# Q, K and V as 49 products of 128 x 128 x 128, and layer norms normalised on ScalarE

## The chip, the cores and the metric

The kernel runs on one core of a Trainium2 chip. A core has a matrix engine (PE in the profile, with the loads of its stationary operand shown apart as PEld), VectorE (DVE), ScalarE (ACT), GpSimd (POOL) and SyncE (SP), which here only starts transfers between HBM and the on-chip SBUF. Matrix products land in PSUM banks of 128 x 512 fp32 and are read from there by DVE or ACT. The metric is the device time of one execution in microseconds.

## The reference

128 graphs of 64 nodes with 512 features pass through four layers, each of the form `x = layernorm(x + layer(x, adj))`, all in fp32: a hypergraph convolution (512 to 1024 to 512), an attention-like layer with one 512 x 512 weight, three graph convolutions of 512 x 512, and graph attention with 8 heads of 64. The change lies in the last one, and in the layer norms of all four:

```python
qkv = (x @ W_qkv).reshape(B, N, HEADS, 3, DIM_HEAD)
q, k, v = (jnp.transpose(qkv[..., i, :], (0, 2, 1, 3)) for i in range(3))
dots = jnp.einsum('bhid,bhjd->bhij', q, k) * scale
...
out = jnp.einsum('bhij,bhjd->bhid', attn, v)
return out @ W_out + b_out
```

## The kernel before

Sixteen groups of 8 graphs (512 rows of `x`, held as four pairs of 128 x 512) go through all layers. In the steady state three groups are in the kernel at once, each in another part of it: `first_half` of group q+1 ("a" in the order lists), the layers of `second_half` of group q ("b"), and the attention's tail of group q-1 ("t", the later part of the same generator). The list `order` at the end of the kernel says in which sequence the pieces are written down for each step. That sequence is the priority: a planner then lays out each engine's queue, and takes for an engine the piece of work that is first in it among those whose operands are ready. `behind(key)` forbids that a piece comes before a named instruction of its engine; `strict` holds for the start and the end only.

Every 512 x 512 x 512 product of a group is written as seven products of 256 x 256 x 256 (`multiply`, `product`, line 539) on four quadrants of either operand: B11, B21 and B22 are quadrants or a sum, T1 to T4 sums. `Left.sums` makes the four sums of the activations (lines 518 to 521, DVE). The sums of the weights are made once, in the first group (`Weight.making`, lines 263 to 268), and kept in DRAM by POOL's transfers (line 280). Products accumulate in three PSUM banks out of a pool of four (`ps_acc`); between two accumulations ACT copies a bank away (`snap`, line 555), DVE adds the copies to later products (lines 568, 589, 598) and ACT copies the last quadrant (line 608). For Q, K and V that is three DVE adds and four ACT copies a product. The stationary operand is always 128 x 128 and the moving one has 256 columns.

`Stream` loads the weights on SP's queue in the order of use (`pump`, lines 236 and 238), into a ring of `RING` = 20 slots of 256 KB; a product of a group beyond the first takes seven slots, one after the other. Activations live in the pool `big` (8 slots), the copies of banks and the softmax tiles in `work` (7).

`layer_norm` takes means and variances on DVE (lines 457 and 458), the root on ACT (line 447), the reciprocal on DVE (line 448) and normalises each pair on DVE (line 463). It is used for the four outer layer norms of every group, except l0 and l1 of the first; `late` pairs are normalised in a second call. The hidden layer norm (line 797) has code of its own.

In `second_half`, after the third graph convolution: `agg` adds into `x`, the layer norm `l2`, transposes (line 1186), ACT copies (line 1194), `left.sums()`, the product q with a stop after five of seven, the addition of the output bias to `x` (line 1201), k, the 64 x 64 `scores` (lines 1356 and 1367), then v, the softmax, and so on. The residual and the layer norm `l1` of the group ahead (`a.p2`, `a.ln1`), and the last layer norm of the group behind (`t.ln3`), lie among them in the order list.

## Time and profile before

| | |
|---|---|
| three executions, us | 2732.28, 2733.82 (median), 2734.45 |
| profiled execution: its span, us | 2732.1 |
| instructions | 67,726 |
| PE busy | 2714.7 us, 28,770 matmuls |
| PEld busy | 2347.7 us, 28,770 loads |
| DVE busy | 2077.8 us, 4,111 |
| ACT busy | 803.9 us, 1,440 |
| POOL busy | 38.0 us, 71 |
| DMA | 405.14 MB, mean 148 GB/s |
| granted PE clock | 1.000 |

The span is the profiled execution from its first to its last instruction; it lies 0.2 us under the fastest of the three times and 1.7 us under their median. Busy time is the union of an engine's instructions. Since instructions of one engine overlap in their pipeline, the distance between two starts says more of what one costs than its duration does. One matmul of the program is two instructions on PE, each with its own load of the stationary operand.

### The profile page before, as it was taken

How to read it: one execution, taken by the hardware profiler on the slowest of the kernel's cores; microseconds unless marked ns; L12 is line 12 of the kernel's file. 1: busy time of each engine (PE TensorE's matmuls, PEld its weight loads, DVE VectorE, ACT ScalarE, POOL GpSimd, SP SyncE). 2: the span in 40 equal slices, each digit the busy share in tenths (PEclk: the TensorE clock that was granted, in tenths of full speed). 3: DMA queues.
4: the chain of work that ended last, by engine and by line, in shares of the span. 5: the costliest groups of instructions: out<-in, count | busy, mean ns of one | idle time of the engine just before them, and what ended most of it. 6: DMA issues, size and time to landing. Idle time of an engine off the chain costs nothing.

```text
span 2732.1 us, 67726 instructions
## 1 busy us (share of the span) xinstructions
PE 2714.7 (99%) x28770; PEld 2347.7 (86%) x28770; DVE 2077.8 (76%) x4111; ACT 803.9 (29%) x1440; POOL 38.0 (1%) x71
## 2 busy tenths in 40 slices
PE   9999999999999999999999999999999999999998
PEld 7888888888888888888888888888888888888887
DVE  6878687876877778777786877778677687776766
ACT  3323223232232332323223233232322323233232
POOL 2000000000000000000000000000000000000000
PEclk9999999999999999999999999999999999999999
DMA  7545454454544545455454554545545455454541
GB/s 257 179 129 154 123 175 140 142 162 131 173 131 139 168 129 170 130 145 168 134 165 129 146 165 133 164 129 151 163 130 167 130 154 157 128 166 129 158 125 63
DMA packets 309532, 405.14 MB, mean 148 GB/s; under 512 B 57424, under 2 KB 185456, under 8 KB 309232
## 3 DMA queue, kind: packets, MB, share of 16 engines
q1 hardware_dynamic: 304256, 385.45, 48.2%
q0 software_dynamic: 4832, 15.24, 1.5%
q8 instruction: 228, 3.74, 0.6%
q14 instruction: 72, 0.59, 0.1%
q10 hardware_dynamic: 144, 0.13, 0.0%
HBM read 369.78 MB, written 30.93 MB: 147 GB/s over the span
## 4 chain that ended last, share of the span: by engine, by line
PE 96%; DVE 3%; ACT 1%; issue 0%; DMA 0%; DVEq 0%
PE a_l0w L539 15%; PE b_l0w L539 7%; PE a_l2b L539 4%; PE a_q L539 4%; PE a_k L539 4%; PE a_l2a L539 4%; PE a_v L539 4%; PE c_l0w L539 4%; PE a_l1w L539 4%; PE a_wo L539 4%; PE a_l2c L539 4%; PE gt_l L481 3%; PE gt_l0h L481 2%; PE b_l2a L539 2%; PE b_l1w L539 2%; PE b_l2b L539 2%
## 5 line engine op out<-in xcount | busy, mean ns | idle before, releaser
L539 PE MATMUL a_l0w<-w2w,aT_l0h 128*128 128x256 f32 x720 | 164.3, 381 | 0.0
L457 DVE BATCH_NORM_STATS2 st_l<-x 128x6 f32<-128x512 f32 x244 | 157.9, 676 | 0.6
L539 PEld LDWEIGHTS a_l0w<-w2w,aT_l0h 128*128 128x128 f32 x720 | 135.6, 190 | 18.8
L463 DVE TENSOR_SCALAR x<-x,mv_l,rs_l 128x512 f32<-128x512 f32 x244 | 119.3, 543 | 2.2
L539 PE MATMUL b_l0w<-w2w,s_l0h 128*128 128x256 f32 x480 | 108.5, 379 | 0.0
L783 ACT ACTIVATE h<-h 128x1024 f32<-128x1024 f32 (+1 forms) x58 | 55.0, 948 | 178.5 <-DVE h L598 157.4
L539 PEld LDWEIGHTS b_l0w<-w2w,s_l0h 128*128 128x128 f32 x480 | 91.1, 190 | 12.5
L1140 ACT ACTIVATE aT_h<-gth,gb_col 128x256 f32<-128x256 f32 x124 | 47.2, 491 | 159.0 <-PE gth L1128 159.0
L447 ACT ACTIVATE rs_l<-mv_l,eps_t 128x4 f32<-128x4 f32 (+1 forms) x63 | 18.8, 298 | 252.3 <-DVE mv_l L458 245.0
L492 ACT COPY aT_l<-gt_l 128x512 f32<-128x512 f32 x148 | 78.1, 597 | 46.4 <-PE gt_l L481 46.4
L555 DVE TENSOR_TENSOR u_l0w<-a_l0w,b_bc 128x512 f32<-128x512 f32 x56 | 38.6, 689 | 69.2 <-PE a_l0w L539 69.2
L539 PE MATMUL a_l2b<-gwbw,aT_h 128*128 128x256 f32 x360 | 86.6, 383 | 0.0
L539 PE MATMUL a_l2c<-gwcw,aT_h 128*128 128x256 f32 x360 | 86.3, 382 | 0.0
L539 PE MATMUL a_q<-aT_xT,wqw 128*128 128x256 f32 x360 | 85.1, 379 | 0.5 <-ACT aT_xT L1194 0.5
L539 PE MATMUL a_l1w<-ww,aT_l 128*128 128x256 f32 x360 | 85.1, 379 | 0.2 <-ACT aT_l L492 0.2
L539 PE MATMUL a_l2a<-aT_l,gwaw 128*128 128x256 f32 x360 | 85.0, 379 | 0.0
L539 PE MATMUL a_k<-aT_xT,wkw 128*128 128x256 f32 x360 | 85.0, 379 | 0.0
L539 PE MATMUL a_v<-wvw,aT_xT 128*128 128x256 f32 x336 | 81.1, 384 | 0.5 <-issue 0.5
L539 PE MATMUL a_l0w<-w1aw,aT_l 128*128 128x256 f32 x336 | 80.8, 383 | 0.0
L539 PE MATMUL a_wo<-wow,aT_oT 128*128 128x256 f32 x336 | 79.5, 379 | 0.0
L539 PE MATMUL a_l0w<-w1bw,aT_l 128*128 128x256 f32 x336 | 79.4, 379 | 0.0
L539 PEld LDWEIGHTS a_l2c<-gwcw,aT_h 128*128 128x128 f32 x360 | 67.2, 190 | 11.6 <-ACT u_l2c L555 3.0
(532 smaller groups left out, 6489.0 us busy)
## 6 DMA issues: line engine op xcount, KB each, us to landing
w2w<-w2k SPq DMA_DIRECT2D x210, 256.0 KB, 2.7
x<-in_x_dram SPq DMA_DIRECT2D x15, 1024.0 KB, 5.8
w1aw<-w1ak SPq DMA_DIRECT2D x60, 256.0 KB, 2.7
w1bw<-w1bk SPq DMA_DIRECT2D x60, 256.0 KB, 2.8
ww<-wk SPq DMA_DIRECT2D x60, 256.0 KB, 2.7
gwaw<-gwak SPq DMA_DIRECT2D x60, 256.0 KB, 3.4
gwbw<-gwbk SPq DMA_DIRECT2D x60, 256.0 KB, 2.7
gwcw<-gwck SPq DMA_DIRECT2D x60, 256.0 KB, 2.7
```

The source lines that it names most:

```text
L447: act.activation(rs[:, at], mv[:, at, 1], AF.Sqrt, bias=eps_t)
L457: vec.bn_stats(st, xg[:, p, :])
L463: vec.tensor_scalar(xg[:, p, :], xg[:, p, :], mv[:, p, 0:1], rs[:, p : p + 1], ALU.subtract, ALU.mult)
L481: ten.matmul(ps[g][f * C : (f + 1) * C, c, p, :], src(2 * duo + p)[rows, c0 : c0 + C], mat[rows, 2 * duo + p, :], start=True, stop=True,)
L492: act.copy(o[:, :, :, g, :], ps[g])
L539: ten.matmul(acc[:, blk, :], lhsT, rhs, start=(first and blk == 0 and i == 0), stop=(last and i == n_k - 1), skip_group_check=True,)
L555: last_add[f"{key}.{what}"] = (act.copy(t, ps) if res is None else vec.tensor_add(t, ps, res(m, n))).ins
L783: act.activation(hn, hn, AF.Relu)
L1140: act.activation(o[:, :, h, :], cols, AF.Relu, bias=gb2_col[:, k : k + 1])
```

## The change

Three things change. First, q, k and v of all groups but the first: each of the seven 256-cubed products is itself written as seven products of 128 x 128 x 128, so 49 for a 512-cubed product. They run in two halves (`DEEP`: four of the outer products, then three); a stage is one inner product for all outer products of a half, four or three matmuls side by side in one bank. `deep_stages` interleaves the halves of q, k and v in one sequence of 42 stages. The inner sums of the activations are made on DVE (`more_sums`), those of the weights on POOL in the first group (`make_deep`), which also writes all seven inner operands to DRAM, so that a stage loads one piece of 256 or 192 KB. Each half ends in quadrants of the outer products, in `temps`, and from these DVE makes q, k or v. Second, `layer_norm` normalises with ACT (`Identity` with a scale and a bias for each row) and DVE computes that bias, `shift`. Third, the pools and the order: `RING` 16, `big` 9, `work` 8, scores after the stage (5, T1), and v in three pieces.

```diff
-RING = 20
+RING = 16
+
+DEEP = ((B11, B21, T1, T2), (T3, T4, B22))
+STAGES = (B11, B21, B22, T1, T2, T3, T4)
+
+
+def deep_stages(n):
+
+    order = [(0, s) for s in (B11, B21, T1, T2, B22)]
+    for i in range(n):
+        if i + 1 < n:
+            order += [(i + 1, B11), (i, T3), (i + 1, T1), (i + 1, B21), (i, T4), (i + 1, T2), (i + 1, B22)]
+        else:
+            order += [(i, T3), (i, T4)]
+    return order
...
-    big = ctx.enter_context(tc.tile_pool(name="big", bufs=8))
+    big = ctx.enter_context(tc.tile_pool(name="big", bufs=9))
-    work = ctx.enter_context(tc.tile_pool(name="work", bufs=7))
+    work = ctx.enter_context(tc.tile_pool(name="work", bufs=8))
...
+        def load_deep(self, q, h, s):
+            n = len(DEEP[h])
+            t = wring.tile([P, 2 * Q], FP, name=f"{self.name}d{h}{s}_{q}", tag="wq")[:, : n * P]
+            nc.sync.dma_start(out=t, in_=self.deep_kept[h][:, STAGES.index(s)].rearrange("p r n -> p (r n)"))
+            return t.rearrange("p (r n) -> p r n", r=n)
...
+        def make_deep(self, got):
+
+            self.deep_kept = []
+            for h, rs in enumerate(DEEP):
+                n = len(rs)
+                k = dram.tile([P, 7, n, P], FP, name=f"{self.name}deep{h}", tag=f"{self.name}deep{h}")
+                d = big.tile([P, 4, n, P], FP, name=f"{self.name}deep_{h}", tag="big")
+                for i, r in enumerate(rs):
+                    b = got[r][0].rearrange("p k (n c) -> p k n c", n=2)
+                    nc.gpsimd.tensor_sub(d[:, 0, i], b[:, 0, 1], b[:, 0, 0])
+                    nc.gpsimd.tensor_sub(d[:, 1, i], b[:, 1, 1], d[:, 0, i])
+                    nc.gpsimd.tensor_sub(d[:, 2, i], b[:, 1, 1], b[:, 0, 1])
+                    nc.gpsimd.tensor_sub(d[:, 3, i], b[:, 1, 0], d[:, 1, i])
+                    nc.gpsimd.dma_start(out=k[:, 0:2, i], in_=b[:, :, 0])
+                    nc.gpsimd.dma_start(out=k[:, 2, i], in_=b[:, 1, 1])
+                nc.gpsimd.dma_start(out=k[:, 3:7], in_=d)
+                self.deep_kept.append(k)
...
-                for what, t in (whole | made if self.scaled else made).items():
+                for what, t in (whole | made if self.scaled else {} if self.deep else made).items():
...
+                if self.deep:
+                    self.make_deep(got)
...
-    w_q, w_k, w_v = (Weight(Wqkv, n * D, f"w{'qkv'[n]}") for n in range(3))
+    w_q, w_k, w_v = (Weight(Wqkv, n * D, f"w{'qkv'[n]}", deep=True) for n in range(3))
...
+                if wt.deep and q > 0:
+                    if wt is w_q:
+                        trio = (w_q, w_k, w_v)
+                        self.todo += [(trio[i // 2], q, (i % 2, s), 1) for i, s in deep_stages(6)]
...
+                if wt.deep and q > 0:
+                    self.here[wt, q, what] = wt.load_deep(q, *what)
...
-        rs = rstd(mv, G, key, slice(pairs[0], pairs[-1] + 1))
+        at = slice(pairs[0], pairs[-1] + 1)
+        rs = rstd(mv, G, key, at)
+        shift = small.tile([P, G], FP, name=f"shift_{key}", tag="shift")
+        vec.scalar_tensor_tensor(shift[:, at], mv[:, at, 0], -1.0, rs[:, at], ALU.mult, ALU.mult)
...
-                vec.tensor_scalar(
-                    xg[:, p, :], xg[:, p, :], mv[:, p, 0:1], rs[:, p : p + 1], ALU.subtract, ALU.mult
+                act.activation(
+                    xg[:, p, :], xg[:, p, :], AF.Identity, bias=shift[:, p : p + 1], scale=rs[:, p : p + 1]
                 )
...
+    class Deep:
+        def __init__(self, key):
+            self.key = key
+            self.xs = [big.tile([P, 8, Q], FP, name=f"d{n}_{key}", tag="big") for n in range(2)]
...
+        def sums(self):
+            self.left = {what: self.slot(what) for what in range(7)}
+            a = self.left
+            s3 = a[T3]
+            vec.tensor_add(a[T1], s3, a[T4])
+            vec.tensor_sub(a[T2], a[T1], a[B11])
+            vec.tensor_sub(s3, a[B11], s3)
+            vec.tensor_sub(a[B22], a[B21], a[T2])
+        def more_sums(self):
...
+            for h, rs in enumerate(DEEP):
+                n = len(rs)
+                o = self.xs[h][:, : 2 * n].rearrange("p (r k) (m c) -> p r k m c", k=2, m=2)
+                s1, s2, s4 = ((x3, st)[h][:, i] for i in range(3))
...
+                vec.tensor_add(s1, o[:, :, 0, 1], o[:, :, 1, 1])
+                vec.tensor_sub(s2, s1, o[:, :, 0, 0])
+                vec.tensor_sub(s4, o[:, :, 1, 0], s2)
+                vec.tensor_sub(s3, o[:, :, 0, 0], o[:, :, 0, 1])
+                self.deep.append({
+                    B11: o[:, :, 0, 0], B21: o[:, :, 1, 0], B22: s4, T4: o[:, :, 1, 1], T1: s1, T2: s2, T3: s3,
+                })
+    def deep_multiply(left, jobs, q):
...
+        banks, snaps, temps = {}, {}, {}
+        for at, s in deep_stages(2 * len(jobs)):
+            j, h = divmod(at, 2)
...
+            bank = "a" if s in (B11, T2, T3, T4) else "b" if s == B21 else "c"
+            fresh, last = s in (B11, B21, T1), s in (B21, B22, T4)
+            if fresh:
+                banks[at, bank] = ps_acc.tile([P, 4, P], FP, name=f"{bank}{h}_{key}", tag="acc")
+            ps = banks[at, bank][:, :n]
+            ws = stream.take_deep(wt, q, h, s)
+            for i in range(n):
+                lhsT, rhs = left.deep[h][s][:, i], ws[:, i]
+                if flipped:
+                    lhsT, rhs = rhs, lhsT
+                ten.matmul(ps[:, i], lhsT, rhs, start=fresh and i == 0, stop=last, skip_group_check=True)
+            stream.done(wt, q, (h, s))
+            if (j, h) not in temps:
...
+            def snap(what):
+                t = work.tile([P, 4, P], FP, name=f"{what}{h}_{key}", tag="w")[:, :n]
+                act.copy(t, ps)
+                snaps[at, what] = t
+
+            if s == B11:
+                snap("u1")
+            elif s == T1:
+                snap("u5")
+            elif s == T2:
+                snap("u2")
+            elif s == B21:
+                vec.tensor_add(sub(0, 0), ps, snaps.pop((at, "u1")))
+            elif s == B22:
+                vec.tensor_add(sub(0, 1), ps, snaps.pop((at, "u2")))
+            elif s == T3:
+                snap("u3")
+                vec.tensor_add(sub(1, 1), snaps.pop((at, "u3")), snaps.pop((at, "u5")))
+            else:
+                act.copy(sub(1, 0), ps)
+                r = {what: temps[j, h][:, i] for i, what in enumerate(rs)}
+                if h == 0:
+                    vec.tensor_add(dst(0, 0), r[B11], r[B21])
+                    vec.tensor_add(dst(1, 0), r[B11], r[T2])
+                    last_add[f"{key}.h"] = vec.tensor_add(dst(0, 1), dst(1, 0), r[T1]).ins
+                else:
+                    last_add[f"{key}.d"] = vec.tensor_add(dst(1, 1), dst(0, 1), r[T3]).ins
+                    vec.tensor_add(dst(0, 1), dst(0, 1), r[B22])
+                    vec.tensor_add(r[T4], r[T4], r[T3])
+                    last_add[key] = vec.tensor_add(dst(1, 0), dst(1, 0), r[T4]).ins
+            yield at, s
...
-        left = Left(f"xT_{q}")
+        left = Deep(f"xT_{q}")
...
+        if q > 0:
+            left.more_sums()
...
+        else:
+            gen = deep_multiply(
+                left, ((w_q, turned(qT), f"q_{q}", True), (w_k, turned(kT), f"k_{q}", True), (w_v, nat(v), f"v_{q}", False)), q
+            )
+            until(gen, 0, B22)
             yield "q1"
+            until(gen, 1, T4)
         with behind(f"q_{q}"):
             vec.tensor_add(xg, xg, bo_bc.unsqueeze(1).to_broadcast([P, G, D]))
         yield "q"
...
+        else:
+            until(gen, 2, T4)
             yield "k1"
+            until(gen, 3, T4)
         yield "k"
+        if q > 0:
+            until(gen, 5, T1)
         probs = [scores(g, duo, qT, kT) for duo in range(2)]
         yield "dots"
...
+        else:
+            until(gen, 5, B22)
             yield "v1"
+            until(gen, 5, T3)
+            yield "v2"
+            whole(gen)
         yield "v"
...
-        gen = multiply([left], (w_v, q), nat(v), f"v_{q}", stops=(3, 6))
-        next(gen)
+        until(gen, 5, B22)
...
-        next(gen)
+        until(gen, 5, T3)
...
-        t.v1 a.c1 t.v b.gt t.soft a.w1a1 a.w1a t.soft2 a.resid b.l2a1 b.l2a a.w1b1 t.ptp a.w1b t.pv a.lnh b.l2b1
+        t.v1 a.c1 t.v2 b.gt t.v t.soft a.w1a1 a.w1a t.soft2 a.resid b.l2a1 b.l2a a.w1b1 t.ptp a.w1b t.pv a.lnh b.l2b1
...
-        t.v1 b.gt t.v t.soft t.soft2 b.l2a1 t.ptp b.l2a t.pv t.osum b.l2b1 b.l2b b.gb3 b.gh b.l2c1 b.l2c2 t.o1 b.l2c t.o2 b.agg
+        t.v1 b.gt t.v2 t.v t.soft t.soft2 b.l2a1 t.ptp b.l2a t.pv t.osum b.l2b1 b.l2b b.gb3 b.gh b.l2c1 b.l2c2 t.o1 b.l2c t.o2 b.agg
```

More of the change, by code (lines that the diff above doesn't have):

```diff
@@ L398, in take, with take_deep @@
             return self.here[wt, q][what]
+        def take_deep(self, wt, q, h, s):
+            self.pump()
+            return self.here.pop((wt, q, (h, s)))
         def done(self, wt, q, what):
-            if q > 0:
+            if wt.deep and q > 0:
+                self.held -= 1
+            elif q > 0:
                 self.held -= wt.halves
@@ L526, in sums, with half, slot @@
             return self
+    class Deep:
+        def __init__(self, key):
+            self.key = key
+            self.xs = [big.tile([P, 8, Q], FP, name=f"d{n}_{key}", tag="big") for n in range(2)]
+        def half(self, m):
+            return self.xs[m][:, 0:4, :]
+        def slot(self, what):
+            m, i = next((m, rs.index(what)) for m, rs in enumerate(DEEP) if what in rs)
+            return self.xs[m][:, 2 * i : 2 * i + 2, :]
+        def sums(self):
[7 more added lines that the diff above has]
+        def more_sums(self):
+            x3 = big.tile([P, 4, 4, P], FP, name=f"d2_{self.key}", tag="big")
+            st = sp.tile([P, 3, 3, P], FP, name=f"ds_{self.key}", tag="s")
+            tail = self.xs[1][:, 6:8, :].rearrange("p k m -> p (k m)")[:, : 3 * P].rearrange("p (r m) -> p r m", r=3)
+            self.deep = []
+            for h, rs in enumerate(DEEP):
+                n = len(rs)
+                o = self.xs[h][:, : 2 * n].rearrange("p (r k) (m c) -> p r k m c", k=2, m=2)
+                s1, s2, s4 = ((x3, st)[h][:, i] for i in range(3))
+                s3 = (x3[:, 3], tail)[h]
+                vec.tensor_add(s1, o[:, :, 0, 1], o[:, :, 1, 1])
[5 more added lines that the diff above has]
+                })
@@ L528, in product, with until @@
+    def until(gen, at, s):
+        while next(gen) != (at, s):
+            pass
     def product(acc, lefts, wt_q, what, first, last, flipped):
@@ L1188, in second_half @@
                             )
[L1189 removed]
+            o = left.half(duo).rearrange("p c (a g i) -> p c a g i", a=2, g=2)
             for h in range(2):
```

36 lines of the change are left out of this document (24 added, 12 removed).

## The prediction

> **What bounds the kernel now.** I read the page first, for busy time and for the chain of work that ended last.
>
> ```profile
> span 2732.1 us, 67726 instructions
> PE 2714.7 (99%) x28770; PEld 2347.7 (86%) x28770; DVE 2077.8 (76%) x4111; ACT 803.9 (29%) x1440; POOL 38.0 (1%) x71
> ...
> PE 96%; DVE 3%; ACT 1%; issue 0%; DMA 0%; DVEq 0%
> ```
>
> PE is the path: 96% of the chain, hardly ever idle, at a granted clock of 1.000. So a change is worth what it takes off PE's stream, less the new places where PE has to wait. Second, the timeline of PE and PEld, for what a matmul costs in the stream (start, length, engine, line, count).
>
> ```profile
> 1402.07 1.70 PEld L539 LDWEIGHTS a_q<-aT_xT,wqw 128*128 128x128 f32 x8
> 1403.80 1.70 PEld L539 LDWEIGHTS a_k<-aT_xT,wkw 128*128 128x128 f32 x8
> ...
> 1418.67 0.30 PEld L539 LDWEIGHTS a_v<-wvw,aT_xT 128*128 128x128 f32 x2
> ...
> 14.64 0.54 PEld L127 LDWEIGHTS dps<-atc,ht 64*64 64x64 f32 x16 [0.33 <-issue]
> ...
> 1416.19 0.49 PEld L696 LDWEIGHTS sps<-hb,ht 64*64 64x64 f32 x14 [0.33 <-issue]
> ```
>
> Eight instructions of 256 columns take 1.73 us from start to start, 216 ns each, although a load lasts 190 and a matmul some 380: both overlap their neighbours. The third line is the first pair after a stall: two loads of 190 ns within 0.30, so the second starts some 110 ns after the first. The last two lines use two 64 x 64 corners of the array in turn, 8 and 7 loads in each. With one moving column (dps) loads follow at (0.54 - 0.135) / 7 = 58 ns in a corner, with 64 columns (sps) at (0.49 - 0.135) / 6 = 59. Third, DVE and ACT in the stretches q, k, then dots to the second graph product, and the rest of a group's period of 168 us (length, then busy time of PE, PEld, DVE, ACT, POOL; clock; DMA).
>
> ```profile
> 1391.90:1404.00 12.10, 12.10 (x57) 10.64 (x56) 11.70 (x24) 2.65 (x5) 0.00 (x0) 1.00 0.55 154
> 1404.00:1416.20 12.20, 12.20 (x59) 10.46 (x57) 8.35 (x17) 2.56 (x5) 0.00 (x0) 1.00 0.71 215
> 1416.20:1435.20 19.00, 19.00 (x457) 16.74 (x457) 14.86 (x26) 8.57 (x15) 0.00 (x0) 1.00 0.58 184
> 1435.20:1559.90 124.70, 124.70 (x1231) 107.76 (x1226) 94.00 (x190) 35.60 (x64) 0.00 (x0) 1.00 0.48 135
> ```
>
> In the stretch that the change fills with additions, DVE is already busy 11.70 of 12.10 us. Fourth, DVE's timeline there.
>
> ```profile
> 1392.29 0.69 DVE L520 TENSOR_TENSOR aT_xT<-aT_xT 128x512 f32<-128x512 f32 x1
> 1392.89 0.69 DVE L521 TENSOR_TENSOR s_xT<-aT_xT,s_xT 128x512 f32<-128x512 f32 x1
> 1393.49 0.75 DVE L870 SCALAR_TENSOR_TENSOR x<-y,rowsum,x 128x512 f32<-128x512 f32 x1
> ...
> 1399.54 1.00 DVE L463 TENSOR_SCALAR x<-x,mv_l,rs_l 128x512 f32<-128x512 f32 x2
> 1400.45 0.69 DVE L568 TENSOR_TENSOR qT<-c_q,u_q 128x512 f32<-128x512 f32 x1
> ```
>
> An addition of 128 x 512 costs 0.60 us from start to start. And the addition of c_q, whose matmuls had ended at 1398.99, stood behind the normalising of `a.p2`, earlier in the list: DVE follows the order written down.
>
> **PE's stream.** A product of q has 28 matmuls, 56 instructions, 56 x 0.216 = 12.1 us. The new one has 49, so 98 instructions with half the columns. No row of before shows 128 columns behind a 128 x 128 load, so it is bounded. Streaming alone: 216 / 2 = 108 ns, and the 110 ns between two loads says the same of the load. The corner rows: 59 ns where streaming would need 216 / 4 = 54, thus 5 ns more, or 1.09 times; at 128 columns 113 or 118. I take 112, by the corner rows, where load and matmul are as long as each other as they would be here, and the 5 ns as a fixed cost: 98 x 0.112 = 11.0 us, 1.1 less, for 45 products (3 in 15 groups) **-50 us**. At 108 it is 10.6, -68; at 118 it is 11.6, -24; level at 123. That a load's whole 190 ns would be the distance is excluded by the pair 110 apart.
>
> [...]
>
> **DVE.** A deep product takes 13 additions: 10 of 512 elements at 0.60, 3 of 384 at an estimated 0.47 (in proportion, plus the fixed part), 7.4 us instead of 3 x 0.60 = 1.8; three make +16.8. `more_sums` adds 4 x 0.60 + 4 x 0.47 = 4.3. Gone are 16 normalisings, four in 1.92 us at 1408.76, so -7.7; four `shift` at some 0.17, the row of the small reciprocals, bring +0.7. Net +14 us a group: 129 of 168 becomes 143 of about 165. As a whole it fits; where it falls, not. In q and k DVE had 20.0 us; less 3.6 of old additions and 3.9 of normalising, plus 14.8 + 4.3 + 0.4, makes 32 beside 22 us of PE. From dots on it is 14.9 - 1.8 + 7.4 = 20.5 beside 18. Twelve us too much, then; but what nobody on PE needs soon is as large: the output bias (2.29, line 1201), the statistics of the last norm (3.2) and the softmax (twelve instructions of 0.60 before 1435, 7.2), which PE needs only at the transposes 30 us later, in a stretch with some 10 us of idle DVE between 1435 and 1463.
>
> What PE waits for is a bank. Three banks of a half live at once, out of four, and the fourth goes to the next half; the eighth stage needs the bank that the first DVE addition frees. DVE starts the sums at 1390.48, and in the order stand sums (3.0 with one of y), `more_sums` (4.3), then `a.p2` with four residual additions (2.74) and statistics (3.2): 1403.7. PE starts q at 1391.92 and comes to stage eight after 6.6 us, at 1398.5: 5 us of waiting if it kept to its sequence. But four further stages (T4 of half 0, T2, T3 and T4 of half 1) and, once T4 has freed its bank, the T1 itself need only banks already held and ACT's copies, 3 to 4 us of work that can be laid before the wait. Thus 1 us remains. The second place, bias and statistics before k's additions (5.5 us), finds three stages (2.4 us) of slack and the same kind of substitute: 0.2 or less. With that **+18 us** for 15 groups; the ends are 0 and the full 5 + 3 us, +120.
>
> **ACT.** Ten copies a product instead of four (five of 0.587, five of an estimated 0.48): +9 us a group; 16 normalisings between 0.63 (line 783) and 0.72 (line 1105), +11: 49 becomes 69 of 165. In the deep stretch a copy has two stages, 1.3 us at least, and needs 0.1 to start and 0.59; one normalising before it is covered, a table load (1283 ns) is not quite. That is within the 18. The norm l2, on whose result the transposes at 1387.65 start, ends some 0.3 us later on ACT; the second half of the transposes hides that.
>
> **Weights, POOL, SP.** A group's q, k and v now load 42 pieces, 21 x 256 + 21 x 192 KB = 9.4 MB instead of 5.4. With the other 2.7 MB or so of that stretch and 39 us it would need 310 GB/s, about what the share 0.71 at 215 GB/s gives for a full queue (303). Sixteen slots (3.6 MB, 12 us of stages) are loaded ahead, so 210 suffice. Cost 0; without the ring's lead it would be 2 us a group. SP starts a piece in 0.32 to 0.46 us, so 42 fit in 39 us. In the first group POOL's chain is 28 small subtractions a weight (0.2 to 0.6, from a fill of 128 columns at 0.205 and a copy of 1,024 at 1.03) and 16 transfers of 0.54, near 17 us, where it had 4 transfers. Made at 200.4, 218 and 236, its ring slots are wanted again at about 226, 238 and 257: **+3 us**, between 0 and 15. Its results are first read by the next group, over 100 us later.
>
> **Sum.** 2732.1 - 50 + 18 + 3 = 2703.1 for the profiled execution; the median of the runs lies 1.7 above its span, so 2704.8, said as **2705 us**.
>
> **The rivals.** (1) *DVE's queue decides*: PE is not given the substitute stages, or ACT's copies for them come late, and loses 6 us a group at the two places above. For it: DVE at 11.70 of 12.10 before anything is added, and its order. Against: 38 us of DVE idle in the period and movable work. 2733.8 - 50 + 90 + 3 = 2777; it decides from (50 - 3) / 15 = 3.1 us a group. (2) *The load does not hide behind 128 columns*: 130 ns, 98 x 0.130 = 12.7, +29 instead of -50, with the same waits 2784. For it: the recorded 190 ns; against: the pair 110 apart and the corners at 59. (3) *Nothing waits*: 108 ns and all additions covered, 2733.8 - 68 + 3 = 2669. (4) *A draw*, gain eaten by waits of 3 us: 2733.
>
> **How the numbers follow.** The forecast 0.52, (1) 0.25, (2) 0.08, (3) 0.10, (4) 0.05. The forecast's own range is 2682 to 2724, from 108 to 118 ns and waits of 0 to 2 us a group. Over the cases 2672 to 2785, which cuts the lower half of (3) and the tails of (1) and (2). What three runs can tell from no change is about 0.2%, 5.5 us: faster 0.62, same 0.05, slower 0.33.
>
> **What the next profile would show.** Right: matmuls of 128 columns whose eight starts lie 0.87 to 0.94 us apart; PE's idle time before q and v in the waits below 30 us in all, mostly for additions that free a bank; DVE near 143 us in a period of 165. Rival 1: hundreds of waits of PE for the additions of `temps`, in the first dozen stages. Rival 2: stages of four matmuls over 0.98 us with nothing awaited. Wrong altogether it would be if a transfer or a slot of `big` held the stages, which nine slots just cover.

## The result and the profile after

The changed kernel takes 2918.0 us (2915.4 to 2925.0), the kernel before 2733.6 in the same series: 1.068 times as long, 95% interval 1.0665 to 1.0695. The forecast of 2705 and its range, up to 2785, were too low. First the page of the profile after: span, busy times, and the shares of the chain that ended last.

```profile
span 2913.3 us, 73634 instructions
PE 2746.0 (94%) x30660; PEld 2406.2 (83%) x30660; DVE 2288.8 (79%) x4498; ACT 1106.9 (38%) x1956; POOL 107.1 (4%) x191
...
PE 74%; DVE 12%; ACT 5%; DMA 5%; issue 2%; POOL 1%; DVEq 0%; ACTq 0%; POOLq 0%; SPq 0%
```

PE was 96% of that chain and is now 74%. The rest is DVE, ACT, transfers and "issue", which together were some 4% before (DVE 3, ACT 1). Next, PE's timeline where q begins (start, length, line, count, wait):

```profile
1468.07 1.05 PE L645 MATMUL a_q<-d_xT,wqd 128*128 128x128 f32 x8
1468.96 1.06 PE L645 MATMUL b_q<-d_xT,wqd 128*128 128x128 f32 x8
1470.42 1.13 PE L645 MATMUL c_q<-d_xT,wqd 128*128 128x128 f32 x8 [0.41 <-PE b_q L645]
...
1477.45 0.94 PE L645 MATMUL c_q<-ds_xT,wqd 128*128 128x128 f32 x6 [0.68 <-ACT v_q L673]
1479.01 0.94 PE L645 MATMUL c_q<-ds_xT,wqd 128*128 128x128 f32 x6 [0.62 <-ACT u_q L656]
```

Eight matmuls of 128 columns start within 0.89 us: 111 ns each, against 112 forecast. The stages themselves are as cheap as hoped; the brackets are the loss. PE's waits of the whole run (total, times, longest), the seven largest (the kernel before has none above 1.3 us in total but 5.3 for `sps`):

```profile
PE a_l2c L701 <- ACT u_l2c L717: 23.7, 15, 2.7
PE gt_l L537 <- DMA x<-in_x_dram: 23.7, 12, 2.8
PE gt_l L537 <- issue: 23.1, 11, 4.0
PE a_v L645 <- DVE v_k L668: 18.0, 15, 1.2
PE c_q L645 <- ACT v_q L673: 9.4, 14, 0.7
PE c_q L645 <- ACT u_q L656: 8.7, 14, 0.6
PE ptp L141 <- DVE sm L141: 7.2, 2, 6.4
```

Four places carry most of it. The windows say where DVE is full (length, then busy PE, PEld, DVE, ACT, POOL; clock; DMA): q and most of k; the rest of k, dots, v and the two graph products; the remainder of the period.

```profile
1468.20:1493.20 25.00, 22.78 (x191) 21.65 (x189) 23.57 (x46) 12.97 (x24) 0.00 (x0) 1.00 0.74 227
1493.20:1523.10 29.90, 23.17 (x506) 21.33 (x505) 23.69 (x46) 14.99 (x27) 0.00 (x0) 0.89 0.66 224
1523.10:1646.60 123.50, 121.99 (x1213) 104.76 (x1211) 93.34 (x188) 40.01 (x70) 0.00 (x0) 1.00 0.44 133
```

DVE is busy 140.6 us of this period of 178.4, near the 143 of the forecast; the period was to be 165. In the first two windows PE loses 9 us, in the third 1.5.

To add up all losses I took, for each pair of matmul instructions, the distance of their starts less the steady distance of that form (216 ns at 256 columns, 111.7 at 128, 14.6 for four 64 x 64 corners in turn, and so on). The steady part went from 2670.3 to 2618.6 us: **-51.7**, the forecast's -50. What is left is PE's lost time; it holds what a lower granted clock adds, too (0.990 over the run after, 1.000 before: at most some 30 us, an estimate, 1% of the span). By the product before which it falls, in us (negative remainders of a form are in "other"; us is the median):

| kernel | us | graph products | q, k, v, dots | 3rd convolution | l0, next products | ptp, pv, pp | other | lost |
|---|---|---|---|---|---|---|---|---|
| before | 2734 | 6.5 | 10.1 | 1.8 | 14.4 | 7.4 | 10.3 | 50.6 |
| after | 2918 | 69.4 | 127.9 | 31.0 | 14.0 | 22.4 | 18.8 | 283.6 |
| b_lnact | 2776 | 9.6 | 16.6 | 33.0 | 14.4 | 7.5 | 12.3 | 93.4 |
| a_lndve | 2903 | 71.1 | 138.2 | 1.8 | 13.6 | 21.6 | 22.7 | 269.1 |
| a_ln0dve | 2890 | 72.4 | 126.6 | 1.9 | 14.2 | 22.3 | 19.9 | 257.3 |
| a_less | 2896 | 88.0 | 98.0 | 29.4 | 11.5 | 16.9 | 19.6 | 263.3 |
| a_less2 | 2851 | 83.3 | 56.2 | 30.9 | 11.5 | 18.5 | 19.3 | 219.7 |
| a_less2_lndve | 2817 | 83.4 | 47.6 | 2.0 | 12.3 | 18.8 | 22.8 | 186.9 |
| a_late_less2 | 2808 | 51.6 | 47.6 | 2.3 | 31.7 | 18.9 | 24.6 | 176.8 |
| a_xp4 | 2928 | 57.5 | 143.3 | 31.0 | 26.4 | 21.3 | 25.0 | 304.4 |
| a_bank5 | 3038 | 113.7 | 86.2 | 29.4 | 32.1 | 31.5 | 111.3 | 404.1 |
| a_order | 2933 | 74.0 | 131.2 | 30.9 | 22.3 | 21.7 | 20.7 | 300.8 |
| a_s2 | 2928 | 19.3 | 142.1 | 29.4 | 51.4 | 30.5 | 21.4 | 294.1 |
| a_s2_lndve | 2914 | 29.4 | 138.7 | 1.9 | 50.9 | 30.7 | 24.7 | 276.3 |
| a_s2_less | 2891 | 22.2 | 113.4 | 30.9 | 43.3 | 25.9 | 21.1 | 256.8 |
| a_s2_less2 | 2845 | 22.6 | 72.7 | 31.0 | 46.2 | 28.2 | 20.8 | 221.6 |
| a_s2_less2_lndve | 2814 | 34.4 | 56.4 | 2.3 | 45.0 | 28.2 | 24.6 | 190.9 |
| b_dense | 2753 | 28.9 | 10.4 | 1.8 | 11.1 | 7.1 | 10.4 | 69.7 |
| a_vonly | 2770 | 22.1 | 27.0 | 1.8 | 15.4 | 20.5 | 14.8 | 101.6 |
| a_vmid | 2750 | 16.9 | 24.5 | 1.8 | 14.9 | 7.9 | 12.8 | 78.8 |

After less before: 233 us more lost, 51.7 less stream, 181.3; the spans differ by 181.2. Names with b_ are variants of the kernel before, those with a_ of the changed one; each comes below. The interval of every ratio to the kernel before is within 0.2% on either side.

### The profile page after: what moved, and what is told of

It reads as the page before. It is cut to its first block, busy times and chain, and to the rows that moved or that the text cites. A ratio compares the mean times of both kernels' runs of the same rounds, so it can differ in the third digit from the quotient of the medians.

```text
span 2913.3 us, 73634 instructions
## 1 busy us (share of the span) xinstructions
PE 2746.0 (94%) x30660; PEld 2406.2 (83%) x30660; DVE 2288.8 (79%) x4498; ACT 1106.9 (38%) x1956; POOL 107.1 (4%) x191
## 4 chain that ended last, share of the span: by engine, by line
PE 74%; DVE 12%; ACT 5%; DMA 5%; issue 2%; POOL 1%; DVEq 0%; ACTq 0%; POOLq 0%; SPq 0%
PE a_l0w L701 12%; PE b_l0w L701 6%; PE a_l2b L701 4%; PE c_l0w L701 4%; PE a_l2a L701 4%; PE a_wo L701 4%; PE gt_l L537 3%; PE a_q L645 3%; PE a_l1w L701 3%; PE a_l2c L701 3%; ACT x L519 3%; DMA out_dram<-x 2%; DMA x<-in_x_dram 2%; DVE st_l L510 2%; PE gt_l0h L537 2%
## 5 line engine op out<-in xcount | busy, mean ns | idle before, releaser
L519 ACT ACTIVATE x<-x,shift_l,rs_l 128x512 f32<-128x512 f32 x246 | 180.3, 803 | 26.8 <-DVE shift_l L515 26.4
L701 PEld LDWEIGHTS a_l0w<-w2w,aT_l0h 128*128 128x128 f32 x720 | 135.6, 190 | 18.8
L645 PE MATMUL a_v<-wvd,d_xT 128*128 128x128 f32 x730 | 103.2, 287 | 22.7 <-DVE v_k L668 18.0
L645 PEld LDWEIGHTS a_v<-wvd,d_xT 128*128 128x128 f32 x730 | 91.0, 196 | 28.0 <-DVE v_k L668 20.9
L645 PE MATMUL a_k<-d_xT,wkd 128*128 128x128 f32 x750 | 104.3, 280 | 5.7 <-ACT u_k L656 5.7
L645 PE MATMUL a_q<-d_xT,wqd 128*128 128x128 f32 x750 | 100.8, 277 | 0.7 <-ACT d_xT L1356 0.3
L645 PEld LDWEIGHTS a_k<-d_xT,wkd 128*128 128x128 f32 x750 | 91.9, 192 | 9.6 <-ACT u_k L656 7.8
L645 PEld LDWEIGHTS a_q<-d_xT,wqd 128*128 128x128 f32 x750 | 92.3, 192 | 4.6 <-ACT u_q L656 2.5
```

Source lines behind the costliest of these rows:

```text
L519: act.activation(xg[:, p, :], xg[:, p, :], AF.Identity, bias=shift[:, p : p + 1], scale=rs[:, p : p + 1])
L645: ten.matmul(ps[:, i], lhsT, rhs, start=fresh and i == 0, stop=last, skip_group_check=True)
L701: ten.matmul(acc[:, blk, :], lhsT, rhs, start=(first and blk == 0 and i == 0), stop=(last and i == n_k - 1), skip_group_check=True,)
```

## The experiments

I set theory W (separate waits, each with its own cause and price) against theory D (DVE, too full from the sums to v, is late, and the rest follows), and later S (PE's instructions arrive too slowly at the graph products).

### The norms on ACT

b_lnact puts them on ACT in the kernel before; a_lndve takes them off ACT in the changed one (its edit is shown, without the lines of `shift`); a_ln0dve takes off l0 alone:

```diff
         def scale(ps):
             for p in ps:
-                act.activation(
-                    xg[:, p, :], xg[:, p, :], AF.Identity, bias=shift[:, p : p + 1], scale=rs[:, p : p + 1]
+                vec.tensor_scalar(
+                    xg[:, p, :], xg[:, p, :], mv[:, p, 0:1], rs[:, p : p + 1], ALU.subtract, ALU.mult
                 )
```

> The kernel before, with one part of the change alone: the layer norms normalise on ACT. In the changed kernel a pass over a pair takes 0.80 us on ACT, four in 2.93 us, where DVE took 1.92. Theory W (separate waits: the loss of the changed kernel is a sum of single waits, each with its own cause and price): ACT's four passes of l0 stand ahead of a copy that frees a bank, 1.7 us a group in the changed kernel; the same place should cost here too, and the later end of l3 eats most of the 1.4 us that the load of x had in hand. 2733 + 15 x (1.7 to 2.3) = 2758 to 2768. Theory D (DVE's load in the stretch of q, k and v is the one cause, and what stands elsewhere follows from it): DVE has 7 us a group less to do, no wait that counts: 2725 to 2736.

> The changed kernel with its second part undone: the layer norms normalise on DVE as before. Theory W: the wait of the third graph convolution's first stages for ACT (1.7 us a group) goes, the chain from the norm l3 to the load of x is 1.0 to 1.4 us shorter, the copies after the norm l3 come 0.5 us earlier; 2918 - 15 x (2.7 to 3.5) = 2866 to 2878. Theory D: DVE has 3.9 us more in the stretch of q and k, where it is short already, and 7 in all; waits for its additions grow by 3 us a group or more: 2960 to 2980. Near 2918 the two would cancel.

> The changed kernel with one of the four layer norms back on DVE, l0, which lies 100 us behind the crowded stretch. In the changed kernel PE waits 23.7 us in 15 places for the copy behind its four passes on ACT. DVE has 1.9 us a group more, at a place where its additions are not waited for. If that wait is a price of its own, all of it comes back: 2918 - 24 = 2894 or a little less. If the whole period is set by the crowded stretch alone, nothing comes back: 2912 to 2920. And all four norms on DVE gave 2903: then the other three must have cost 9 us there.

Measured: 2775.9 us (ratio 1.0155, 1.014 to 1.017), 2902.7 and 2890.5. This part alone slows the kernel before by 43 us. That is 8 above W's range and far from D's: the third convolution loses 31 us more, where W had 25, and q, k, v and dots 6.5. a_lndve lies between the two ranges. The three largest waits of PE in b_lnact:

```profile
PE a_l2c L542 <- ACT u_l2c L558: 24.0, 15, 2.7
PE sps L127 <- DVE hb L127: 5.3, 1, 5.3
PE gt_l L484 <- issue: 3.2, 4, 1.7
```

The same place in the timeline of the changed kernel, ACT and then PE:

```profile
1609.43 2.93 ACT L519 ACTIVATE x<-x,shift_l,rs_l 128x512 f32<-128x512 f32 x4 [0.44 <-DVE shift_l L515]
1612.26 0.56 ACT L717 COPY u_l2c<-a_l2c 128x512 f32<-128x512 f32 x1
...
1612.88 0.48 PE L701 MATMUL a_l2c<-gwcw,s_h 128*128 128x256 f32 x1 [1.51 <-ACT u_l2c L717]
```

l0's four passes stand ahead of the copy that frees PE's bank. On DVE again, l0 gives back 27.5 us (2918.0 to 2890.5), the whole wait: W, at a place 100 us behind the stretch of q, k and v. All four norms on DVE give only 15.4, in the main because the loss in that stretch, where DVE now has more to do, grows by 10 (127.9 to 138.2 in the table).

### DVE's additions

a_less leaves out the last three of the seven additions that make q, k and v (1.8 us of DVE a product); a_less2 also `more_sums`; a_less2_lndve is that with the norms on DVE.

```diff
-                    vec.tensor_add(dst(0, 1), dst(0, 1), r[B22])
-                    vec.tensor_add(r[T4], r[T4], r[T3])
-                    last_add[key] = vec.tensor_add(dst(1, 0), dst(1, 0), r[T4]).ins
...
-                vec.tensor_add(s1, o[:, :, 0, 1], o[:, :, 1, 1])
...
+                s1, s2, s3, s4 = o[:, :, 0, 1], o[:, :, 1, 1], o[:, :, 0, 0], o[:, :, 1, 0]
```

> The changed kernel without the last three of the seven additions that make q, k and v from the inner results (the sums of two quadrants are left incomplete): DVE has 1.8 us less to do for each product, 5.4 us a group, and nothing else changes. Theory D: DVE works without a pause from the sums on; with 1.8 us less before them the bias and the statistics of l3 end early enough, so PE's waits for the additions of k (1.4 us a group) and for the first stages of k (0.9) go, and x is written and loaded 1.8 to 3.6 us earlier (1.5 to 2.3): 2918 - 15 x (3.5 to 4.6) = 2849 to 2866. Theory W: DVE's amount does not matter, only which operation stands ahead of which: 2905 to 2918.

> As the run before without the last three additions of q, k and v (2896), and also without the eight additions of more_sums (views of the outer operands stand in their place; results are wrong). DVE has 9.7 us a group less than in the changed kernel, and near the end of the sums 4.3 us less. Theory D (DVE's backlog through the stretch from the sums to the first products of the next step): the residual, the statistics of l1 and l3 and every addition of q come 4.3 us earlier, the load of x too; 2896 - 15 x (1.5 to 3) = 2850 to 2875. Theory W (the remaining waits are for ACT's copies, the instruction supply and x's load, each by itself): 2885 to 2900.

> The changed kernel in its own order, without the three additions behind q, k and v and without more_sums (the sums are left incomplete), and with the layer norms on DVE: the DVE of the kernel before plus 4 us a group, ACT with its copies alone. If what is left is the supply of instructions and the load of x at the graph products (47 us in the run without the additions), the two ends (some 20) and the copies in front of the next product's stages (some 30), then 2851 less the 24 to 28 us of the wait before the third convolution: 2815 to 2827. If the norms on ACT cost only what they cost in the changed kernel, 2836.

Measured: 2896.4, 2850.8 and 2817.3. Busy times of a_less2:

```profile
PE 2727.2 (96%) x30660; PEld 2409.3 (85%) x30660; DVE 2149.8 (75%) x4243; ACT 1103.9 (39%) x1956; POOL 106.6 (4%) x191
```

With 139 us less work for DVE PE loses 64 us less, and in q, k, v and dots 72: D, there. Most telling is q alone, whose waits are named after ACT's copies and a bank: its loss falls from 41.9 to 7.6 us when `more_sums` goes, although ACT does the same as before. DVE's timeline of the changed kernel shows why:

```profile
1473.92 2.73 DVE L1032 SCALAR_TENSOR_TENSOR x<-y,rowsum,x 128x512 f32<-128x512 f32 x4
1476.57 1.27 DVE L510 BATCH_NORM_STATS2 st_l<-x 128x6 f32<-128x512 f32 x2
...
1479.16 0.65 DVE L666 TENSOR_TENSOR v_q<-b_q,u_q 128x512 f32<-128x512 f32 x1
...
1479.83 0.65 DVE L668 TENSOR_TENSOR v_q<-c_q,u_q 128x512 f32<-128x512 f32 x1
```

The matmuls of `b_q` and `c_q` had ended at 1470.0 and 1473.8, but the additions that free their banks stand behind `more_sums`, the residual and most of the statistics. So PE, at 1477.45 and 1479.01, could go on only in banks that ACT's copies freed. a_less, the first step, missed both ranges (2896; D 2849 to 2866, W 2905 to 2918): the wait for `a_v` went as D expected, but the graph products lost 19 us more. The norms are worth 33.5 us here, where DVE has room, instead of 15.4.

### One more bank

a_bank5 has five PSUM banks for products and three for graph products, dots and transposes.

> The changed kernel with five PSUM banks for the products and three for the graph products, dots and transposes (it was four and four). The stages of q wait 2.4 us a group for copies and additions that free a bank. If the number of banks is what limits them, this goes: 2918 - 15 x (1.5 to 2.4) = 2882 to 2896, more if the first stages of k and v gain as well, less what the graph products lose with three banks (bounded by nothing that a row shows; each writes two banks a time). If DVE's pace is what limits them, the same work waits at the next stage: 2910 to 2930.

3038.1 us, far above both ranges. The loss before q falls from 41.9 to 16.3 us, so the banks are indeed what q's stages meet; but everything that now has three banks loses more. Part of that is the clock, granted at 0.979 instead of 0.990 (at most some 34 us, an estimate from the spans). As a remedy it fails; the share of banks in the loss before q it does show.

### The two graph products: x, and the supply of instructions

The chain that leads to them in the changed kernel (DVE, ACT, SP's queue, PE):

```profile
1488.45 0.68 DVE L683 TENSOR_TENSOR qT<-qT,v_q 128x512 f32<-128x512 f32 x1
1489.05 2.28 DVE L1374 TENSOR_TENSOR x<-x,bo_bc 128x2048 f32<-128x2048 f32 x1
1491.25 1.28 DVE L510 BATCH_NORM_STATS2 st_l<-x 128x6 f32<-128x512 f32 x2
...
1493.85 0.66 DVE L668 TENSOR_TENSOR v_k<-c_k,u_k 128x512 f32<-128x512 f32 x1
...
1496.23 2.93 ACT L519 ACTIVATE x<-x,shift_l,rs_l 128x512 f32<-128x512 f32 x4
...
1499.19 0.39 SPq L1428 DMA_DIRECT2D out_dram<-x  x1
1505.06 0.37 SPq L167 DMA_DIRECT2D x<-in_x_dram  x1
...
1504.96 1.61 PE L1540 MATMUL dot<-kT,qT 64*64 64x64 f32 x92
...
1511.11 1.97 PE L537 MATMUL gt_l<-smat,x 64*64 64x64 f32 x118 [1.44 <-DMA x<-in_x_dram]
1516.73 0.69 PE L537 MATMUL gt_l<-smat,x 64*64 64x64 f32 x10 [3.65 <-issue]
1517.34 1.65 PE L645 MATMUL a_v<-wvd,d_xT 128*128 128x128 f32 x6
1518.92 3.50 PE L537 MATMUL gt_l<-atc,x 64*64 64x64 f32 x128
```

The same place in the kernel before, with the load of `x` and PE's dense runs (128 matmuls of 64 x 64 pieces each):

```profile
1416.83 0.38 SPq L153 DMA_DIRECT2D x<-in_x_dram  x1
...
1416.70 2.04 PE L1356 MATMUL dot<-kT,qT 64*64 64x64 f32 x126
1418.67 1.99 PE L539 MATMUL a_v<-wvw,aT_xT 128*128 128x256 f32 x8
...
1424.05 2.09 PE L481 MATMUL gt_l<-smat,x 64*64 64x64 f32 x128
1426.07 1.99 PE L539 MATMUL c_v<-wvw,aT_xT 128*128 128x256 f32 x8
...
1433.18 2.10 PE L481 MATMUL gt_l<-atc,x 64*64 64x64 f32 x128
```

`x` has three buffers, so the load of one group waits until another's output is written, that until l3 is normalised, and that until DVE has come past q's last additions. In the kernel before, the load was issued at 1416.83, landed 5.8 us later, and the product began at 1424.05 without a wait; now PE stands. Then, 118 of 128 matmuls in, it stands 3.65 us more with nothing awaited. a_xp4 gives `x` a fourth buffer (`work` shrinks from 8 to 6 to make room):

> The changed kernel with four buffers for x instead of three, so that the load of the group after next does not wait for the output transfer of a group before; to make room, the pool work has 6 buffers instead of 8. Theory W: PE's wait of 2.3 us a group for the load of x goes: 2918 - 15 x 2.3 = 2884, less if the two missing buffers hold up copies. Theory D: the wait for x comes from DVE's lateness, and PE then waits for DVE or ACT within the next stages instead: 2905 to 2920. If the instruction stalls follow from PE's stop at x, they go too: down to 2850.

2928.1 us, above both ranges. The wait for x is gone, and nothing is won; the waits for an addition of k grow instead (18.0 us in the changed kernel). How much of this is due to the two buffers that `work` lost was not separated:

```profile
PE gt_l L537 <- issue: 27.5, 16, 3.7
PE a_v L645 <- DVE v_k L668: 27.4, 15, 1.9
```

Three changes of the order list (a_order exchanges `t.v` and `b.gt`; a_s2, shown here, takes `b.gt` first and the product with x 7 us later; a_late_less2 moves `b.gt` behind the next product's first stages, with DVE relieved):

```diff
-        t.v1 a.c1 t.v2 b.gt t.v t.soft a.w1a1 a.w1a t.soft2 a.resid b.l2a1 b.l2a a.w1b1 ...
+        t.v1 b.gt t.v2 t.v b.l2a1 a.c1 t.soft b.l2a a.w1a1 a.w1a t.soft2 a.resid a.w1b1 ...
```

> The changed kernel with one pair exchanged in the order: the last stages of v stand before the graph product of the third layer's input (t.v before b.gt) instead of after it, so that two graph products of 64 x 64 pieces no longer follow one another. Theory W with a cause in the supply of instructions: PE stands 2.9 us a group within the two graph products with nothing awaited (issue); with the stages of v between them the queue can fill, and half to all of it goes: 2918 - 15 x (1.4 to 2.9) = 2875 to 2897. Theory D: the same work of DVE in the same stretch, 2910 to 2920.

> The changed kernel with another sequence behind the dots: first the graph product of group b (which needs no load), the rest of v and the first stages of its next product, and only then the graph product of the group ahead, which needs x from HBM. So the load of x has some 7 us more, and 5 us of wider matmuls lie between the two dense runs of 64 x 64 pieces (128 instructions and 128 loads in 1.9 us each). In the changed kernel these two runs cost 2.3 us a group waiting for x and 2.9 with nothing awaited (issue). Theory W (separate waits) with supply of instructions as the cause of the second: both go, 2918 - 15 x (3.9 to 5.2) = 2840 to 2860. Theory D (DVE is late and everything else follows): PE comes earlier to work that DVE has not prepared, and waits for it: 2900 to 2920.

> The kernel without the last three additions, without more_sums and with the layer norms on DVE (2817), and with one item moved in the order: the graph product of group b behind the first stages of the next group's first product, so that some 5 us of wide matmuls lie between the two dense runs, where it was 0.7. The first dense run still follows the dots by 2.9 us. PE's loss in the two runs was 51.9 and 31.5 us. Theory S (supply of instructions): the second goes, the first stays: 2817 - (20 to 30) = 2787 to 2797. If the loss at the graph products has another cause (the load of x, the busy transfers), or the sequence gives it back elsewhere as the other one did: 2810 to 2825.

a_order (2933.0) hardly moved PE's queue: the planner set v's last stage into the second graph product instead of behind it and left the rest, so it tells nothing of S; it came out 13 us above D's range and 36 above W's. a_s2 took 50 us away at the graph products, as W and S said, and came to 2927.9: the next products lost 37 more, q to dots 14, ptp and pv 8. Is that DVE's lateness? Four more runs with this sequence say no:

> The same sequence with the layer norms normalising on DVE as before. On its own the latter gave 2903, with 65 us more loss at the two graph products than the kernel before. Theory W: 50 to 65 us of it go, 2838 to 2853. Theory D: DVE has 7 us a group more than in the run beside it; at least half of what is gained comes back at the additions of k and v: 2870 to 2903.

> The sequence with the two graph products apart (2928 by itself) together with the leaving out of the three additions (2896 by itself, against 2918). If the two effects are separate, they add: 2928 - 22 = 2906. Theory D: the other sequence took 50 us of waits away at the graph product, and PE gave them back waiting for DVE's late additions of v, sums and softmax; with 5.4 us less on DVE it keeps a good part of them: 2918 - 22 - (20 to 50) = 2846 to 2876.

> The same sequence without the three additions and without more_sums: DVE has 9.7 us a group less, so it works about as much as in the kernel before plus 4 us. Theory D: nearly all that waits for DVE goes (a_v, b_k, a_k, the start of l2a and of the second half of l0, 6 to 7 us a group in the run with this sequence): 2928 - 15 x (6 to 8) = 2808 to 2838. Theory W: 2885 to 2906. What stays in either are the wait for ACT before the third convolution (1.7 a group), the first stages of q (2.4), and the two ends.

> The run with the same sequence and without the eleven kinds of additions, and the layer norms on DVE as before: DVE's load is then that of the kernel before and 10.7 us of it. ACT has no normalising left. The wait before the third convolution (24 to 26 us) goes; if DVE now has room for the 7 us a group, 2808 to 2838 becomes 2780 to 2815. If DVE is still the limit, no gain against the run beside it. That the wide-to-narrow change of the matmuls themselves saves 3.4 us a group is seen only here: with nothing waiting it would end at 2733 - 50 + the ends (17) = 2700.

2914.0, 2890.7, 2845.5 and 2814.3: with DVE relieved or not, the next products lose 43 to 51 us. The first two miss both theories' figures, the third lies 7 us above D's, the last at the end of its range. So the sequence itself makes these waits, and the total does not tell what the graph products gained. The cleanest test of S leaves the change out. b_dense is the kernel before with `b.gt` ahead of `t.v`, so that the two dense runs touch:

```diff
-        t.v1 a.c1 t.v b.gt t.soft a.w1a1 ...
+        t.v1 a.c1 b.gt t.v t.soft a.w1a1 ...
```

> The kernel before, with one pair exchanged in its order: the graph product of group b directly behind that of the group ahead, the last four stages of v behind both. Nothing of the change is in it: no inner products, no normalising on ACT, no more weights. Theory S (supply of instructions): PE's instructions come in blocks of 16 KB, at least 3.5 us apart in the traces; a dense run of 64 x 64 pieces uses one up in 1.9 us, and two in a row empty the store. Then PE stands with nothing awaited (issue) in these two runs, 1.5 to 3.5 us a group as in the changed kernel: 2734 + 16 x (1.5 to 3.5) = 2758 to 2790. Rival: the stalls of the changed kernel come from its own weight traffic or from PE's earlier stop at x; then this kernel shows none: 2730 to 2740.

2752.6 us (1.0068, 1.0053 to 1.0083). PE's timeline:

```profile
1603.66 2.09 PE L481 MATMUL gt_l<-smat,x 64*64 64x64 f32 x128
1605.57 1.34 PE L481 MATMUL gt_l<-atc,x 64*64 64x64 f32 x46
1608.48 1.44 PE L481 MATMUL gt_l<-atc,x 64*64 64x64 f32 x82 [1.57 <-issue]
```

The stall comes without any part of the change, though 19 us is less than the 24 to 56 expected. That it is the supply is seen in the transfers of the kind "instruction": all 13 stops of over 0.5 us inside the graph products of this run ended 2.2 to 2.9 us after such a block had started, and all eleven in the changed kernel 2.3 to 2.6 us. With this the runs show S at work, as far as that queue is PE's (it is inferred, see the last section). And a_late_less2, with 5 us of wide matmuls between the runs, loses 6.0 us in the second one instead of 31.5. It ends at 2808.3, 9 us better and not 20 to 30, because the next product lost 19 more.

### Inner products for v alone

a_vonly keeps q and k as seven products of 256 cubed, writes `more_sums` behind k, spreads v's stages around the graph products and normalises on DVE; a_vmid further leaves out the last group and spreads v's stages seven, five, two instead of five, seven, two. The line in which both begin:

```diff
-    w_q, w_k, w_v = (Weight(Wqkv, n * D, f"w{'qkv'[n]}", deep=True) for n in range(3))
+    w_q, w_k, w_v = (Weight(Wqkv, n * D, f"w{'qkv'[n]}", deep=n == 2) for n in range(3))
```

> The changed kernel with the inner products for v alone, q and k as seven products of 256 cubed, more_sums written down behind k, the layer norms on DVE, and v's stages spread between dots and the two graph products (five stages, seven, two). PE's stream gains 15 x 1.15 = 17 us. DVE has 9.9 us a group more than in the kernel before (4.3 + 5.6), but all of it behind k, where the kernel before left DVE idle for some 15 us. Theory D with S (the loss of the changed kernel comes from the crowded stretch of q and k and from the dense runs too near to each other): both are eased here, 2717 to 2740. If a deep product costs its waits wherever it stands, a third of the changed kernel's 236 us of lost gain: 2734 - 17 + 60 to 80 = 2777 to 2797.

> The kernel with the inner products for v alone (2770), further without them in the last group, whose tail took 15 us more with them, and with v's stages spread seven, five, two around the graph products, so that PE comes to x and to the second dense run later. In that kernel a steady group took some 1 us more than in the kernel before, the first group 5. If the rest of its loss is x and the two dense runs (18 us) and the last group (15): 2770 - 33 = 2737, between 2726 (waits all gone: 2734 - 14 x 1.15 + 5 + 3) and 2750. Only if it ends under 2728 would a version with inner products beat the kernel before by more than the measurement is uncertain.

2770.0 us (1.0136, 1.0119 to 1.0153) and 2750.0 (1.0059, 1.0046 to 1.0072); the first lies between its two ranges, the second at the upper end of its own. The stream is 17 and 16 us shorter, the lost time 51 and 28 longer. The crowded stretch is no longer the reason (q and k lose some 5 us); v and dots lose 19 to 22 and the graph products 10 to 16 more. So no version with inner products that I ran beats the kernel before.

## Why the prediction was wrong

In the terms of the sum: the stream's -50 measured -51.7. The +18 for waits of q, k and v measured +118 (127.9 less 10.1 in the table). Places that the sum put at nothing came to +63 (graph products), +29 (third convolution), +15 (`ptp`, `pv`, `pp`) and +8 (the rest); the +3 for the first group lies within these rows. Together that is the 181 us between the spans. So two steps failed: the price of DVE's lateness, and the assumption that nothing outside q, k and v would wait.

**PE's stream: right.** 112 ns and -50 us; measured 111 and -51.7. Rival 2, with 130 ns and +29 us, is out with it.

**DVE's amount: right; what PE waits for it: mis-sized.** 143 us were forecast for a group, 140.6 measured. The forecast let 1.2 us a group remain of 5 + 3 of waiting, because substitute stages could be laid before the wait and because bias and statistics were "movable". Averaged over eleven steady groups, before c_q PE loses 2.4 us, before the stages of k and the first of v 2.6: 5.0, or 75 us in 15 groups. The other 43 stand before later stages of v, at the dots and in the first and last groups. The substitutes were used, but each of them needs a bank freed by an ACT copy behind a late addition, and meets a wait of its own. And nothing moved the bias: in the timeline above it and the statistics of l3 stand ahead of k's additions, as they are written. That is rival 1 in place and nearly in price (6 us a group); it decides from 3.1.

**ACT: the step looked in one place only.** That one normalising before a copy "is covered" was argued for the deep stretch. It was not asked at l0, where four passes stand ahead of the copies of the third convolution: 27.5 us by a_ln0dve. A pass was costed at 0.63 to 0.72 us and takes 0.80 (803 ns, the mean of 246).

**What the prediction had no step for: the graph products.** They lose 63 us more. The load of x hung on l3 by a chain through DVE, ACT and two transfers with some 1.4 us in hand; the forecast followed the norms to PE's transposes, never to the output and the next load. And v's wide stages, which had kept the two dense runs 5.4 and 7.1 us behind what went before, shrank to 3.1 and 0.7. The prediction's last sign was "if a transfer or a slot of `big` held the stages": a transfer held PE, but that of x and not of a weight. That all of the 63 us come from these two causes is not shown (see what stays open).

**The ends.** For the first group +3 was forecast, for its ring slots. Its q starts 1.9 us later than before, and no wait of PE names a slot. But its k then stands 3.9 us for an ACT copy behind four passes of a norm; these had waited for a `shift` of 3.45 us on DVE (0.15 in a later group), at a time when POOL made the sums of a weight. Why it took so long was not looked into. POOL's chain took some 23 us a weight (107.1 less 38.0, by three) and not 17. The last group took some 24.5 us more (its period 9, what follows 15), with nothing forecast; `ptp` waits 7 us there for DVE's softmax, and the granted clock is 0.50 for 17 us from 2877 on. Without inner products in the last group (a_vmid against a_vonly) the loss at ptp, pv and pp falls from 20.5 to 7.9 us, and what follows its q from 75.2 to 63.2, as in the kernel before (63.3).

**The weights: right.** No stage of q, k or v waits for one; the share of DMA in q and k is 0.74.

What stays open: a_less2_lndve loses 136 us more than the kernel before on a stream 52 shorter, and 77 of them at the graph products (37 from q to dots, 11 at ptp, pv and pp). That S is part of it is shown. But before nine of the eleven stops of the changed kernel two blocks of instructions lay 7.4 to 10.6 us apart, in b_dense 3.5 to 6.4: so the blocks themselves came later there, for a reason that was not looked for. How the rest divides between S, the load of x and transfers that were busy 0.98 of the time just before the stall was not separated, and no sequence tried recovered it in the total.

## What to carry to other kernels

An engine's load, added up over a period, does not say whether it fits: DVE was busy 141 us of 178, but 47 of them lay in the 55 us from q to the second graph product, and taking 9.7 us a group off it there gave 64 us back. Where a step becomes shorter, ask what its length had covered: here the supply of instructions between two dense runs and the load of the next input. And moving work to an idle engine must be checked at every place where that engine's queue feeds PE, not only where the change is.

## What the runs showed of the hardware

PE's instructions came in blocks of 16,384 bytes (244 in the changed kernel, for 61,320 matmuls and loads, so some 250 each; that this queue of the kind "instruction" is PE's is inferred from this count and from the stops above). In the traces of before, after, b_lnact and b_dense two blocks started at least 3.3 us apart (3.42 before, 3.33 after, where the expectation for b_dense had 3.5), while a dense run of 64 x 64 pieces, 128 matmuls and 128 loads, uses one up in 1.9. In the run of the changed kernel shown above a block started at 1504.8 and the next at 1514.3, 1.2 us after PE had run dry; PE went on at 1516.7. In four groups, three apart, the stall came after 108, 113, 118 and 123 matmuls of the run, a steady step, as blocks of fixed size would give.

The granted clock was 0.50 for 6.8 us, from 1515.2 on, 2.1 us after PE had run dry and 1.5 before it went on. Windows around it (length, then busy time of PE, PEld, DVE, ACT, POOL; clock; DMA):

```profile
1510.00:1514.00 4.00, 1.97 (x118) 1.86 (x118) 3.98 (x8) 2.62 (x5) 0.00 (x0) 1.00 0.98 354
1514.00:1518.00 4.00, 1.27 (x13) 1.16 (x14) 2.18 (x4) 1.25 (x3) 0.00 (x0) 0.65 0.09 32
1518.00:1522.00 4.00, 4.00 (x121) 3.77 (x124) 3.06 (x5) 1.88 (x4) 0.00 (x0) 0.50 0.20 66
1522.00:1526.00 4.00, 4.00 (x44) 3.60 (x37) 2.04 (x4) 1.48 (x4) 0.00 (x0) 0.99 0.23 70
```

The second graph product took 3.5 us there instead of 2.1. So a stall of 3.65 us cost some 5. In the kernel before the granted clock is 1.000. The clock fell at shorter stops too: with one of 2.72 us, which ended at 358.2, it was 0.50 from 358.1 to 361.5, and in b_dense, after one of 1.81 us, which ended at 928.6, from 929.0 to 932.4. Of the 14 stops with nothing awaited at the graph products of b_dense, only this one was followed by a lower clock. What decides whether it falls is not shown.
